# Program-text order on all five engines, and a DFT column transform in 64 x 64 quadrants

## The chip, the core and the metric

The kernel runs on one core of one Trainium2 chip. The metric is the device time of one execution in microseconds. A core has five engines that run side by side, each through a queue of its own: PE (TensorE, matrix multiplies; its weight loads are shown apart as PEld), DVE (VectorE), ACT (ScalarE), POOL (GpSimd) and SP (SyncE, which here only issues transfers). They wait for each other through semaphores. Within one queue the instructions start in the order in which the program was built.

## The reference, cut to what matters

The input is a float32 batch of 32 images of 96 channels and 56 x 56 pixels. Two layers follow.

```
layer 0: h = silu(bn(conv1x1(x, 96 -> 576)));  d = silu(bn(depthwise3x3(h)))
         s = sigmoid(W2 silu(W1 mean(d)));      x1 = x + bn(conv1x1(d * s, 576 -> 96))
layer 1: mag  = |rfft2(x1)|                     (per channel, 56 x 29)
         ca   = gate per channel, from weighted sums of mag
         sa   = gate per pixel, from mean(x1), l2(x1) and the resized mean of mag
         y    = x1 * ca * sa
         fq   = resized mean over channels of |rfft2(y)|
         off, gate = 3x3 convolutions of [y, coordinates, fq]
         z    = (1 - gate) * conv3x3(y) + gate * deformable3x3(y, off)
         out  = relu(batchnorm(z) + x1)
```

Each image needs two DFTs of all 96 channels, one of x1 and one of y. A DFT is a transform of rows and then a transform of columns, both done as matrix products, followed by the square root of the sum of two squares.

## The kernel before

**Streams.** `layers` interleaves three streams by hand. The main loop goes over 32 images x 7 bands of 8 rows; a band is two halves, and each half samples 7 column blocks of 4 x 4 pixels (`sample_tiles`, L714 on PE and its evictions L718 on ACT), packs nine taps into seven (`pack`, L725) and contracts them (`deform`, L733). Beside it run two generators: `hidden` of the image after next (expansion L166, activation L170, nine depthwise taps per unit on DVE at L255 to L259, and `finish`, L219), and `attend` of the next image (squeeze L282 to L294, projection L321 and L327, and all of layer 1 up to `fq`). `pump` is called once for each column block and three times more at the end of a band, so 70 times for an image, and advances both generators so that each is through when it is due; a generator stands still at each `yield`. `later` holds short pieces that are due some slots on.

**Order.** The generators fix the order of the program text. The body of `layers` lies in `tc.manual_schedule(engines={SP})`: SP's queue keeps the text's order, while PE, ACT, DVE and POOL are ordered by a list scheduler, which may move an instruction ahead of or behind its neighbours in the text as far as data allow. One ACT instruction, L663, is pinned to the text by `keep_in_program_order`.

**The two transforms.** `dft_mag` takes two channels at a time. The row transform (L383) multiplies the pixels of a channel pair by `FU`; the result has two channels x 56 columns on 112 partitions in `s1`. The column transform (L404) multiplies `s1` by a block-diagonal 112 x 112 matrix `GV`, which holds the 56 x 56 cosine (or sine) matrix twice and zeros elsewhere. Three steps of 16 channel pairs each make eight matmul records of 464 columns. ACT squares the two results from PSUM (L406), DVE adds them (L407), and one square root over all follows (L410). The buffer `sq` exists once, and in the first DFT it also holds the sums of L369 until L395 has read them.

**The small chain.** After the first DFT come short dependent steps, each waiting for the one before on another engine: `sums` to L470, L471 and L472; `m_fe` (L420) to L423; `mas` and `qs` (L478 to L490) to L494; L500; L505; L512 with L514; L524 to L528; L533 with L534; L540 with L542; L544 to L549. All of the PSUM tiles of this chain come from one pool `acc` with a single buffer.

**Buffers.** Six PSUM banks `mm` rotate among everything else on PE; `pd` exists once.

Of the kernel before, what the change touches and what calls it, by code (L numbers as in the profile page):

```python
# [24 lines left out]
V = W // 2 + 1  # L25
# [35 lines left out]
NG = C // 2 // CG  # L61
KG = 3
# [273 lines left out]
def dft_mag(nc, p, src, gate=None):  # L336

    w = p["w"]
    hwc = src.rearrange("c (h w) -> h c w", h=H)
    s1 = p["s1p"].tile([2 * W, NP, 2 * V], FP, name="s1")
    if gate is None:
        parts = p["sq"].tile([2 * W, 2, NPB * V], FP, name="sq")[:, :, : NG * W].rearrange("p k (g w) -> p k g w", g=NG)  # L350
    x2s = []

    def load(g):
        if g < NG:
            x2 = p["x2"].tile([2 * H, CG, W], FP, name="x2")
            for half in range(2):
                c0 = half * C // 2 + g * CG
                nc.sync.dma_start(x2[half * H : (half + 1) * H], hwc[:, c0 : c0 + CG])
            x2s.append(x2)

    def weigh(g):
        if gate is not None and g < NG:
            nc.gpsimd.tensor_tensor(x2s[g], x2s[g], gate.unsqueeze(1).to_broadcast([2 * H, CG, W]), ALU.mult)

    def sums(g):
        sq = bank(p)[: 2 * H, : CG * W].rearrange("h (c w) -> h c w", c=CG)
        nc.scalar.activation(sq, x2s[g], AF.Square)
        for k, t in enumerate((x2s[g], sq)):
            nc.vector.tensor_reduce(parts[:, k, g], t.rearrange("h c w -> h w c"), AX.X, ALU.add)  # L369

    for g in range(3):
        load(g)
    for _ in range(2):
        yield
    weigh(0)
    weigh(1)
    yield
    if gate is not None:
        yield
    for g in range(NG):  # L380
        pt = bank(p)
        for i in range(CG // 2):
            nc.tensor.matmul(pt[: 2 * W, i * 4 * V : (i + 1) * 4 * V],  # L383
                             x2s[g][:, 2 * i : 2 * i + 2, :].rearrange("h c w -> h (c w)"), w["FU"],
                             start=True, stop=True)
        if gate is None:
            sums(g)
        weigh(g + 2)
        load(g + 3)
        nc.scalar.copy(s1.rearrange("p (h q) u -> p h q u", h=2)[:, :, g * CG // 2 : (g + 1) * CG // 2],  # L390
                       pt[: 2 * W, : 2 * CG * V].rearrange("p (q h u) -> p h q u", h=2, u=2 * V))
        yield
    if gate is None:
        p["sums"] = p["sp"].tile([2 * H, 2, W], FP, name="sums")
        nc.vector.tensor_reduce(p["sums"], parts.rearrange("p k g w -> p k w g"), AX.X, ALU.add)  # L395
    mag = s1[:, :, :V]
    for j in range(0, NP, NPB):
        n = NPB * V
        sq = p["sq"].tile([2 * W, 2, n], FP, name="sq")
        cos, sin = s1[:, j : j + NPB, :V], s1[:, j : j + NPB, V:]  # L400
        for part, first, second in ((0, (0, cos), (1, sin)), (1, (0, sin), (2, cos))):
            pt = bank(p)
            for k, (g, m) in enumerate((first, second)):
                nc.tensor.matmul(pt[: 2 * W, :n].rearrange("p (q u) -> p q u", q=NPB), w["GV"][:, g], m,  # L404
                                 start=(k == 0), stop=(k == 1))
            nc.scalar.activation(sq[:, part], pt[: 2 * W, :n], AF.Square)  # L406
        nc.vector.tensor_tensor(mag[:, j : j + NPB], sq[:, 0].rearrange("p (q u) -> p q u", q=NPB),  # L407
                                sq[:, 1].rearrange("p (q u) -> p q u", q=NPB), ALU.add)
        yield
    nc.scalar.activation(mag, mag, AF.Sqrt)  # L410
    p["magnitude"] = mag


def resized_spectrum(nc, p, mag, name, scale=None):


    m2 = p["sp"].tile([2 * W, V], FP, name=f"m_{name}")
    if scale is not None:
        nc.vector.tensor_tensor(mag, mag, scale.unsqueeze(2).to_broadcast([2 * W, NP, V]), ALU.mult)
    nc.vector.tensor_reduce(m2, mag.rearrange("p q u -> p u q"), AX.X, ALU.add)  # L420
    yield
    pf = p["acc"].tile([128, 512], FP, name="acc")
    nc.tensor.matmul(pf[:V, : 2 * W], m2, p["w"]["RT2"], start=True, stop=True)  # L423
    rs = p["sp"].tile([V, 2, W], FP, name=name)
    nc.scalar.copy(rs.rearrange("p m w -> p (m w)"), pf[:V, : 2 * W])
    p["resized"] = rs
    yield


def attend(tc, p, b, x, h2d, pooled, x1, given=False):  # L430
# [45 lines left out]
    mas = p["sp"].tile([2 * W, 2, NP], FP, name="mas")  # L476
    edge = p["sp"].tile([2 * W, NP, NE], FP, name="edge")
# [3 lines left out]
    for m in range(2):  # L481
        we = p["sp"].tile([2 * W, NP, NE], FP, name="we")
        nc.vector.tensor_tensor(we, edge, w["wa"][:, m], ALU.mult)
        nc.vector.tensor_reduce(mas[:, m], we, AX.X, ALU.add)


    qs = p["sp"].tile([2 * W, 2, 3, NP], FP, name="qs")
    for m in range(2):
        nc.vector.tensor_tensor(qs[:, m], mas[:, m].unsqueeze(1).to_broadcast([2 * W, 3, NP]), w["wb"][:, m], ALU.mult)
# [16 lines left out]
    c2 = p["sp"].tile([2 * MID, 2 * W], FP, name="c2")  # L506
# [5 lines left out]
    nc.tensor.matmul(pc[: 2 * W, 64 : 64 + NP], c2, w["cp2X"], start=True, stop=True)  # L512
    cx = p["sp"].tile([2 * W, NP], FP, name="cx")
    nc.vector.tensor_tensor(cx, pc[: 2 * W, 64 : 64 + NP], w["cp2bX"], ALU.add)  # L514
# [119 lines left out]
def offsets(nc, p, yp, j, top, hid, ybs, hds):  # L634
# [28 lines left out]
    p["tc"].keep_in_program_order(nc.scalar.activation(ht, ht, AF.Abs, bias=w["blk"]))  # L663
# [115 lines left out]
def constants(tc, ctx, a, p, gather=False):  # L779
# [63 lines left out]
    wa = cp.tile([2 * W, 2, NP, NE], FP, name="wa")  # L843
    wb = cp.tile([2 * W, 2, 3, NP], FP, name="wb")
    gb = cp.tile([C, 3], FP, name="gbias")
    with tc.tile_pool(name="l1w", bufs=1) as wp:
# [7 lines left out]
        ap, bp, fdh, fdw = temp("apad", 2 * W), temp("bpad"), temp("fdhX"), temp("fdwX")  # L854
        ta = wp.tile([2 * W, NP, NE], FP, name="ta")
        tb = wp.tile([2 * W, 3, NP], FP, name="tb")
        for m in range(2):
            for d in range(7):
                first = d == 0
                oa, ob = (wa[:, m], wb[:, m]) if first else (ta, tb)  # L860
                nc.vector.tensor_tensor(oa, ap[:, m, d].unsqueeze(1).to_broadcast([2 * W, NP, NE]),
                                        fdh[:, :, d : d + 1].to_broadcast([2 * W, NP, NE]), ALU.mult)
                nc.vector.tensor_tensor(ob, bp[:, m, :, d : d + 1].to_broadcast([2 * W, 3, NP]),
                                        fdw[:, :, d].unsqueeze(1).to_broadcast([2 * W, 3, NP]), ALU.mult)
                if not first:
                    nc.vector.tensor_tensor(wa[:, m], wa[:, m], ta, ALU.add)
                    nc.vector.tensor_tensor(wb[:, m], wb[:, m], tb, ALU.add)
# [41 lines left out]
def padded(nc, p, a, images):  # L909
# [3 lines left out]
    for t in yps:  # L913
        nc.gpsimd.memset(t, 0.0)
        nc.sync.dma_start(t[C : C + 4, PD : PD + H, PD : PD + W], a["coord"])
        nc.sync.dma_start(t[CA:, PD : PD + H, PD : PD + W], a["place"])
    p["s4"] = [cp.tile([H, 3, WP], FP, name=f"s4_{i}") for i in range(2)]
# [11 lines left out]
def layers(tc, a, dp, x1d, zd, stats, far):  # L929
# [8 lines left out]
    with ExitStack() as ctx:  # L938
# [7 lines left out]
        pools(tc, ctx, p, None, (("xt", 2), ("acch", 2), ("pl", 2), ("w3s", 1), ("hq", 1), ("o", 2), ("x2", 3),  # L946
# [290 lines left out]
def gather_block(tc, a, dp, x1d, zd, stats):  # L1237
# [4 lines left out]
    with ExitStack() as ctx:  # L1242
# [11 lines left out]
        pools(tc, ctx, p, None, (("x2", 3), ("ca", 1), ("s1p", 1), ("xc", 2), ("sp", 1), ("sq", 2), ("q1", 2), ("q2", 2),  # L1254
# [77 lines left out]
def body(ctx, tc, a, out):  # L1332
# [8 lines left out]
    with tc.manual_schedule(engines={mybir.EngineType.SP}):  # L1341
# [8 lines left out]
def _arrays(inp):  # L1350
# [39 lines left out]
    A["cp1"] = np.ascontiguousarray(cp1.reshape(2 * MID, 3, NP, 2).transpose(2, 1, 3, 0))  # L1390
    cp2 = l1["cp2_w"].reshape(NP, 2, MID)
    A["cp2X"] = np.ascontiguousarray(cp2.transpose(1, 2, 0).reshape(2 * MID, NP))
    A["cp2bX"] = np.ascontiguousarray(np.repeat(l1["cp2_b"].reshape(NP, 2).T, W, 0))
    A["twoT"] = np.kron(np.eye(2), np.ones((MID, W))).astype(f)
# [8 lines left out]
    for k in range(1, KA):  # L1403
# [13 lines left out]
    A["GV"] = np.ascontiguousarray(np.stack(  # L1417
        [np.kron(two, np.cos(t)), np.kron(two, np.sin(t)), np.kron(two, -np.sin(t))], 1).astype(f))
    A["two"] = np.kron(two, np.ones((W, 1))).astype(f)
# [8 lines left out]
    apad, bpad = np.zeros((1, 2, 7, V), f), np.zeros((2, W, 2, 3, 7), f)  # L1428
    for d in range(7):
# [3 lines left out]
        bpad[:, -np.arange(V), 1, :, d] = bp[:, 6 - d : 6 - d + V].T[:, None]  # L1433
# [4 lines left out]
    A["apad"], A["bpad"] = ends, bpad.reshape(2 * W, 2, 3, 7)  # L1438
    A["bsum"] = np.stack([bp[:, 6 - d : 6 - d + V].sum(1) for d in range(7)], -1).astype(f)[None]
    pairs = lambda v: np.repeat(v.reshape(NP, 2, 7).transpose(1, 0, 2), W, 0)  # L1440
# [7 lines left out]
    RT2 = np.zeros((2, W, 2, W), f)  # L1448
    RT2[:, np.arange(V), 0] = RT / C
    RT2[:, -np.arange(V), 1] = RT / C  # L1450
    A["RT2"] = RT2.reshape(2 * W, 2 * W)
# [37 lines left out]
```

## Time and profile before

| | |
|---|---|
| time, median of 3 runs | 9672.42 us (9670.12 to 9673.45) |
| profiled execution | 9701.68 us; span of its instructions 9699.9 us |
| PE busy | 8626.3 us, 89% of the span |
| DVE busy | 7237.3 us, 75% |
| ACT busy | 5341.9 us, 55% |
| POOL busy | 2531.2 us, 26% |
| mean granted TensorE clock | 0.932 |
| first matmul of `hidden` | at 75.29 us |

A row of a group of instructions gives line, engine, operation, out<-in with shapes and count, then the busy time of the group in us and the mean time of one in ns, then how long the engine had been idle just before them and whose end released it. A float32 matmul stands in the trace as two MATMUL records. Records overlap, so busy time divided by count is less than the mean time of one. The waits list gives engine, line and what it waited for, then the total in us, the number of times and the longest in us. A timeline row gives start, duration and number of records, with the idle time before them in brackets.

### The profile page before, as it was taken

To read this page: it belongs to the slowest core of one execution; us is meant where nothing else is said; L and a number is where in the kernel's file an instruction comes from. 1 tells how busy PE (TensorE), PEld (TensorE's weight loads), DVE (VectorE), ACT (ScalarE), POOL (GpSimd) and SP (SyncE) were. 2 spreads that over 40 slices of the span, in tenths; PEclk is the share of its full clock that TensorE was granted. 3 is DMA by queue.
4 is the path that set the end of the run, shared out by engine and by line. 5 is a ranking of instruction groups with operands and counts; after the bars stand their busy time and mean duration, and the time that the engine had idled before them with its cause. 6 is when DMAs were issued, how large, how long until landed. Compare 5 with 4: busy or idle time off the path is not lost. (4 is left out here: it accounts for less than half of the span.)

```text
span 9699.9 us, 120622 instructions
## 1 busy us (share of the span) xinstructions
PE 8626.3 (89%) x43766; PEld 5004.7 (52%) x43766; DVE 7237.3 (75%) x6948; ACT 5341.9 (55%) x10262; POOL 2531.2 (26%) x2639
## 2 busy tenths in 40 slices
PE   6889999999999999999999999999999999999970
PEld 3455555555555555555555555555555555555540
DVE  7688777777877777787777787777778777777323
ACT  2355555555555556555555555555555555555453
POOL 0133222222222232222222222233222223322210
PEclk9899999999999999999999999999999999999985
DMA  2345555554555555555555555555545555554449
GB/s 94 107 136 143 160 153 157 157 153 138 140 158 152 157 149 148 140 144 150 153 158 154 139 139 155 153 157 155 152 138 143 151 157 157 153 146 135 128 152 417
DMA packets 1069310, 1485.39 MB, mean 153 GB/s; under 512 B 590406, under 2 KB 839958, under 8 KB 1056422
## 3 DMA queue, kind: packets, MB, share of 16 engines
q1 hardware_dynamic: 858747, 985.20, 37.3%
q10 hardware_dynamic: 153675, 329.79, 9.1%
q0 software_dynamic: 56288, 162.60, 6.8%
q8 instruction: 352, 5.77, 0.3%
q14 instruction: 248, 2.03, 0.1%
HBM read 1064.28 MB, written 412.65 MB: 152 GB/s over the span
## 5 line engine op out<-in xcount | busy, mean ns | idle before, releaser
L259 DVE SCALAR_TENSOR_TENSOR acch<-hp,w,acch 128x1512 f32<-128x1512 f32 (+1 forms) x2250 | 4314.4, 1918 | 32.8
L598 PE MATMUL mm<-yp,c_jointW 104*128 104x448 f32 x4032 | 1648.5, 561 | 6.2 <-DMA yp<-fqd 3.4
L733 PE MATMUL pd<-v,c_def 128*96 128x224 f32 (+1 forms) x6272 | 1435.2, 380 | 174.5 <-ACT v L725 147.9
L696 POOL COPY ybl<-yp 96x448 f32<-96x448 f32 x896 | 1016.6, 1161 | 2002.3 <-PE mm L700 1996.8
L733 PEld LDWEIGHTS pd<-v,c_def 128*96 128x96 f32 (+1 forms) x6272 | 1065.3, 175 | 487.7 <-ACT v L725 186.7
L166 PE MATMUL mm<-xt,w 96*128 96x392 f32 (+3 forms) x2688 | 1117.2, 553 | 132.6 <-ACT yt L702 95.9
L714 PE MATMUL mm<-wc,yt 64*96 64x144 f32 x12544 | 1113.9, 301 | 119.1 <-ACT v L718 59.3
L598 PEld LDWEIGHTS mm<-yp,c_jointW 104*128 104x128 f32 x4032 | 785.1, 196 | 802.7 <-issue 760.1
L685 DVE TENSOR_TENSOR wc<-wc,wr 128x1008 f32<-128x1008 f32 x448 | 559.3, 1248 | 776.4 <-DMA wr<-hd 767.9
L219 ACT ACTIVATE acch<-acch,sh,inv 128x1568 f32<-128x1568 f32 x288 | 487.4, 1692 | 1159.2 <-DVE acch L259 1141.5
L714 PEld LDWEIGHTS mm<-wc,yt 64*96 64x96 f32 x12544 | 847.7, 162 | 442.9 <-issue 197.7
L718 ACT COPY v<-mm 96x288 f32<-96x288 f32 (+1 forms) x2688 | 1003.1, 441 | 127.9 <-PE mm L714 85.6
L170 ACT ACTIVATE hp<-mm,sh,inv 128x392 f32<-128x392 f32 (+2 forms) x1216 | 811.6, 672 | 329.4 <-PE mm L166 280.8
L626 PE MATMUL mm<-yp,c_base0W 96*64 96x448 f32 x4032 | 914.6, 551 | 0.0
L321 PE MATMUL mm<-hq,w3s 128*96 128x392 f32 x2048 | 789.9, 532 | 126.5 <-DMA hq<-h2d 124.2
L648 POOL DMA_DIRECT2D od<-at x224 | 185.9, 830 | 2257.6 <-DVE at L644 1483.9
L725 ACT COPY v<-v 32x448 f32<-32x448 f32 x1344 | 755.1, 562 | 29.7
L404 PE MATMUL mm<-s,c_GV 112*112 112x464 f32 x1536 | 662.9, 573 | 0.0
L166 PEld LDWEIGHTS mm<-xt,w 96*128 96x128 f32 (+1 forms) x2688 | 390.5, 187 | 513.8 <-issue 289.8
L702 ACT COPY yt<-mm 128x384 f32<-128x384 f32 (+1 forms) x896 | 351.1, 441 | 463.9 <-PE mm L700 462.0
L321 PEld LDWEIGHTS mm<-hq,w3s 128*96 128x96 f32 x2048 | 336.9, 173 | 478.6 <-issue 374.4
L626 PEld LDWEIGHTS mm<-yp,c_base0W 96*64 96x64 f32 x4032 | 295.3, 135 | 527.8 <-issue 487.9
(193 smaller groups left out, 8959.1 us busy)
## 6 DMA issues: line engine op xcount, KB each, us to landing
h2d<-acch ACTq DMA_DIRECT2D x288, 784.0 KB
wc<-hd SPq DMA_DIRECT2D x896, 252.0 KB
wr<-hd SPq DMA_DIRECT2D x896, 252.0 KB
hq<-h2d SPq DMA_DIRECT2D x128, 980.0 KB
hq<-h2d SPq DMA_DIRECT2D x128, 784.0 KB
x<-x1d SPq DMA_DIRECT2D x768, 98.0 KB
ht<-od SPq DMA_DIRECT2D x224, 252.0 KB
hd<-ht ACTq DMA_DIRECT2D x224, 252.0 KB
```

Of the source, the lines that this page charges most:

```text
L166: nc.tensor.matmul(pt[p0 : p0 + w1.shape[1], : rows * W], w1, xts[hf][:, r0 * W : (r0 + rows) * W], start=True, stop=True)
L170: nc.scalar.activation(h1[lo:hi, row0 : row0 + rows, 1 : 1 + W], pt[lo:hi, : rows * W].rearrange("p (h w) -> p h w", h=rows), AF.Silu, bia ...
L259: nc.vector.scalar_tensor_tensor(acc[:, lo:hi], win, wk, acc[:, lo:hi], ALU.mult, ALU.add)
L321: nc.tensor.matmul(pts[half][:C, :EW], w3s[:, ch], hq, start=(i == 0), stop=False)
L404: nc.tensor.matmul(pt[: 2 * W, :n].rearrange("p (q u) -> p q u", q=NPB), w["GV"][:, g], m, start=(k == 0), stop=(k == 1))
L598: nc.tensor.matmul(view, weights[:, k], yp[:channels, r0 : r0 + RB, dx + PD - 1 : dx + PD - 1 + W], start=(k == 0), stop=(k == NTAP - 1))
L626: nc.tensor.matmul(pb[k % 2 * BC : (k % 2 + 1) * BC, :BW].rearrange("p (h w) -> p h w", h=RB), w["base"][:, k], yp[:C, r0 : r0 + RB, dx + ...
L696: nc.gpsimd.tensor_copy(yb[:, :, s], blocks)
L714: nc.tensor.matmul(pt[k][:C, (t - lo) * KP : (t - lo + 1) * KP], yt[ps, t], s[ps, t * KP : (t + 1) * KP], start=True, stop=True)
L718: nc.scalar.copy(v[:C, :, lo:hi, k].rearrange("c k t p -> c t k p"), pt[k][:C, : (hi - lo) * KP].rearrange("c (t k p) -> c t k p", t=hi - ...
L725: nc.scalar.copy(v[C:, 1 + 2 * i : 3 + 2 * i], v[i * QC : (i + 1) * QC, KA:])
L733: nc.tensor.matmul(out.rearrange("c q (t x) -> c t q x", x=TS), p["w"]["def"][ks, k], v[ks, k].rearrange("c t s (r x) -> c t (s r) x", r=T ...
```

## The change

It does two things.

First, `manual_schedule` is called without a set of engines, so that PE, ACT, DVE and POOL, too, keep the order of the program text. The pin on L663 goes, since it says the same. The text itself, with its yields and slots, stays, but for what follows.

Second, the column transform is done in quadrants. `s1` gets 2 x 64 partitions in place of 2 x 56; the source buffers `x2` are padded to 64 columns with zeros and are kept for the whole program, in place of a pool of three. `GV` becomes a plain 56 x 56 matrix (padded to 64) on either half of the partitions. Each step takes 2 x 2 groups of 8 channel pairs; a matmul uses 64 rows and 64 columns of the array and 232 moving columns, and four of them that follow each other lie in four different quadrants. The two row halves write two different PSUM banks. A step has 16 matmuls (32 records) in place of 4 (8 records), and there are three steps as before (in the diff NQB = 8 and WX = 64). The squares, the sums of squares, the square root and all that is computed from `mag` run on 128 partitions in place of 112, with constants ordered to match.

```diff
-        x2 = p["x2"].tile([2 * H, CG, W], FP, name="x2")
+        x2 = p["x2"][p["n_x2"] % len(p["x2"])]
+        p["n_x2"] += 1
...
-    for j in range(0, NP, NPB):
-        n = NPB * V
-        sq = p["sq"].tile([2 * W, 2, n], FP, name="sq")
-        cos, sin = s1[:, j : j + NPB, :V], s1[:, j : j + NPB, V:]
-        for part, first, second in ((0, (0, cos), (1, sin)), (1, (0, sin), (2, cos))):
-            pt = bank(p)
-            for k, (g, m) in enumerate((first, second)):
-                nc.tensor.matmul(pt[: 2 * W, :n].rearrange("p (q u) -> p q u", q=NPB), w["GV"][:, g], m,
-                                 start=(k == 0), stop=(k == 1))
-            nc.scalar.activation(sq[:, part], pt[: 2 * W, :n], AF.Square)
-        nc.vector.tensor_tensor(mag[:, j : j + NPB], sq[:, 0].rearrange("p (q u) -> p q u", q=NPB),
-                                sq[:, 1].rearrange("p (q u) -> p q u", q=NPB), ALU.add)
+    n = NQB * V
+    pairs = mag.rearrange("p (r q) u -> p r q u", r=2)
+    for q0 in range(0, NP // 2, NQB):
+        sq = p["sq"].tile([2 * WX, 2, 2, n], FP, name="sq")
+        pts = bank(p), bank(p)
+        for part, first, second in ((0, (0, 0), (1, V)), (1, (0, V), (2, 0))):
+            for t, (g, u0) in enumerate((first, second)):
+                for r, k in ((0, 0), (1, 1), (0, 1), (1, 0)):
+                    rows = slice(r * WX, r * WX + W)
+                    q1 = k * NP // 2 + q0
+                    nc.tensor.matmul(pts[r][k * WX : (k + 1) * WX, part * n : (part + 1) * n].rearrange("p (q u) -> p q u", q=NQB),
+                                     w["GV"][rows, g], s1[rows, q1 : q1 + NQB, u0 : u0 + V], start=(t == 0), stop=(t == 1))
+        for r, pt in enumerate(pts):
+            nc.scalar.activation(sq[:, r].rearrange("p k n -> p (k n)"), pt[:, : 2 * n], AF.Square)
+        nc.vector.tensor_tensor(pairs[:, :, q0 : q0 + NQB], sq[:, :, 0].rearrange("p r (q u) -> p r q u", q=NQB),
+                                sq[:, :, 1].rearrange("p r (q u) -> p r q u", q=NQB), ALU.add)
...
-    p["tc"].keep_in_program_order(nc.scalar.activation(ht, ht, AF.Abs, bias=w["blk"]))
+    nc.scalar.activation(ht, ht, AF.Abs, bias=w["blk"])
...
-    with tc.manual_schedule(engines={mybir.EngineType.SP}):
+    with tc.manual_schedule():
         layers(tc, a, dp, x1d, zd, stats, far)
```

Lines move by 2 in `hidden`, by 3 in the row transform and by 7 from `resized_spectrum` to the constants: L166 becomes L168, L219 L221, L404 L410, L406 and L407 L413 and L414, L420 L427, L512 L519, L524 L531, L533 L540, L540 L547, L714 L721, L725 L732, L733 L740.

## The prediction

> **What bounds the kernel now.** I read the page's engine rows first, then the row of the granted clock, the groups by line, PE's waits, and the timeline of one image. Engines and clock:
>
> ```profile
> PE 8626.3 (89%) x43766; PEld 5004.7 (52%) x43766; DVE 7237.3 (75%) x6948; ACT 5341.9 (55%) x10262; POOL 2531.2 (26%) x2639
> PEclk9899999999999999999999999999999999999985
> ```
>
> PE is busy 8626 of 9700 us. Its last matmul ends at about 9411 and its first starts at 75.29; in between it idles about 695 us, 21.5 us for each of 32 images. PE is the bound, so two things can move the time: its work, and its holes. DVE at 75% has slack on average, but a wait behind two or three of its long instructions is long. The clock row never says 10: in the records the clock is full or half, half for about 30 us per image, after holes of 2 to 5 us. Now the groups that the change touches or resembles:
>
> ```profile
> L598 PE MATMUL mm<-yp,c_jointW 104*128 104x448 f32 x4032 | 1648.5, 561 | 6.2 <-DMA yp<-fqd 3.4
> L714 PE MATMUL mm<-wc,yt 64*96 64x144 f32 x12544 | 1113.9, 301 | 119.1 <-ACT v L718 59.3
> L626 PE MATMUL mm<-yp,c_base0W 96*64 96x448 f32 x4032 | 914.6, 551 | 0.0
> L404 PE MATMUL mm<-s,c_GV 112*112 112x464 f32 x1536 | 662.9, 573 | 0.0
> ```
>
> Busy divided by count: L404 takes 0.432 us per record of 464 columns. L598, of nearly L626's columns with the whole array, takes 0.409; L626, with two column halves side by side, takes 0.227, a factor of 0.555. And PE's longest waits:
>
> ```profile
> PE pd L733 <- ACT v L725: 147.9, 71, 6.9
> PE mm L321 <- DMA hq<-h2d: 124.2, 30, 7.9
> PE mm L166 <- ACT yt L702: 95.9, 40, 5.4
> PE acc L423 <- DVE m_fe L420: 43.9, 32, 1.9
> PE acc L524 <- DVE cx L514: 23.7, 29, 1.4
> ```
>
> Waits behind ACT are waits for ACT's order. The small chain costs almost nothing: 1.4 us per image at L423, 0.7 at L524. The timeline of PE shows why:
>
> ```profile
> 4257.65 0.47 PE L700 MATMUL mm<-c_ident,ybl 96*128 96x96 f32 x3 [0.88 <-ACT sq L406]
> 4262.63 1.68 PE L166 MATMUL mm<-xt,w 96*128 96x392 f32 x2 [2.03 <-ACT yt L702]
> 4265.46 0.55 PE L423 MATMUL acc<-c_RT,m_fe 112*29 112x112 f32 x2 [1.16 <-DVE m_fe L420]
> ...
> 4292.59 0.31 PE L524 MATMUL acc<-thT,s 56*56 56x56 f32 x2 [0.39 <-DVE cx L514]
> 4292.83 1.00 PE L733 MATMUL pd<-v,c_def 128*96 128x224 f32 x4
> 4293.76 0.30 PE L524 MATMUL acc<-thT,s 56*56 56x56 f32 x2
> 4293.99 1.00 PE L733 MATMUL pd<-v,c_def 128*96 128x224 f32 x4
> ```
>
> Between two steps of the chain the scheduler has put a matmul of another stream, so ACT evicts the one step while PE works.
>
> **The quadrants.** They remove L404's 662.9 us. There are now 64 DFTs x 3 steps x 32 = 6144 records of 232 columns. One alone should take 0.432/2 = 0.216, so without overlap the work doubles to 1327. Two at a time, with L626's factor: 0.120 each, 737 in all, 74 more than now. Four at a time, with 0.28, about half that factor: 0.060 each, 370 with some 35 us for the switches of tile shape around each step (64 x 3 x 2 switches at 0.09 us; around L714 the first group of a new shape starts 211 ns after the last in place of 122). Gain 293, at best 331.
>
> A rule speaks against this. L626's column halves share all their rows, and its records pair off without an exposed weight load. The Trainium skill, "TensorE: Matmul & The Clock Gate" (What overlaps and what doesn't), says that a weight load passes a running matmul only if their row groups differ. Here two of the four quadrants share a row group, and weights change at every matmul. By the rule about 0.07 us of load would stand bare in each record and the quadrants would cost nearly 6144 x 0.13 = 800, a loss of about 140; by L626's row they gain. I take the row: same rows, loads of the same size, nothing exposed. The switch itself is a drain by "TensorEngine Tiling (Array Packing)" (Key Properties), which gives no figure; the 0.09 us of the trace is used.
>
> ACT's squares stay 2 x 3 per DFT, DVE's sums too; more partitions cost no time. -293.
>
> **The order, start.** ACT's constant loads now stand in text order: some that were issued at 2.6 us come behind two square roots and 19 more loads. SP's first `xt` load waits for `thM`, now built by one chain of DVE steps rather than by interleaved ones. First matmul at 95 to 100 us in place of 75.29: +22.
>
> **The order, after the first DFT.** (Lines here and below are those of before.) In the text PE's next work, a hidden unit's expansion and L423, stands behind L420, DVE's reduction. DVE has ahead of it, from the last L369 on: the four steps of `z` (0.68, 0.80, 0.66, 0.62, each starting before the last ends, 2.2 in all), L395 1.3, three L407 at 0.6, one L685 at 1.2, six taps L259 at 1.95 and one L257 at 1.0 (12.7), then L420 2.6. That is 21.8; small instructions between them 1.0, and waits for ACT's squares 1.5: 24.3. PE's own work over that stretch is 13.9. So PE stands 10.4 us there, once per image (between 5 and 14: how far DVE is ahead when the stretch begins decides). Before, the same stretch has 0.88 + 0.27 + 2.03 + 1.16 = 4.3. In steady state there are 31 images: 31 x 6.2 = +192.
>
> **The order, around the resize of the gates.** In the text L505, L512, two L524, L526 and L527 stand in one block on PE, then one L166 and six L714, then three L533, nine L540 and L549 in one block. No deformable contraction lies between them as it did in the timeline above. Each waits for ACT's eviction of the one before, from a single `acc` buffer. And ACT in the text has L219 and more between the last L528 and the first L534. Step by step, by rows of before: rest of a DVE tap 1.5; the `z` chain ahead of `cx` on DVE 2.7 with its waits; L514 0.2; two L524 with their evictions L528, 0.31 + 0.30 twice, and L515's 0.24, 1.4; L526 and L527 with theirs 0.8; on ACT L219 1.69 + 0.19, L170 0.68, three L725 at 0.56 and two L718 at 0.4 to 0.5, 5.1; three evictions L534 0.9; the last three L540 and L542 0.8; two L546 0.5: 13.9. Ten hops from engine to engine at 0.24 (L524's matmul ends at 4292.90, its eviction starts at 4293.19) make 16.3. PE's own work is 3.6. Stall 12.7 us (9 to 16), before 0.4: 31 x 12.3 = +381.
>
> **Other waits.** New: the second L423 after its own reduction (1.2), the squeeze L288 (0.5), L700 behind POOL's L696 (2.4), less some 1.4 that go: 31 x 2.6 = +80 (0 to 150). Gone: L733's wait for L725 (147.9), since in the text the packs stand where they are needed; and of L166's for `yt` and L714's for `v`, outside the stretch above, some 70: -218 (-100 to -350). The wait of L321 for `hq` (124) is one for data by DMA; SP's order is unchanged, and I leave it.
>
> **The clock.** A hole of 3.46 us slowed the next L321 from 2.87 to 4.54 us:
>
> ```profile
> 5027.84 2.87 PE L321 MATMUL mm<-hq,w3s 128*96 128x392 f32 x8
> 5035.86 4.54 PE L321 MATMUL mm<-hq,w3s 128*96 128x392 f32 x8 [3.46 <-DMA hq<-h2d]
> ```
>
> Holes go and others come; I take nothing, and +-104 (3.3 us an image) for the range. The tail of 288 us after PE (the normalisation) has one order by data in both: nothing.
>
> **Sum.** -293 + 22 + 192 + 381 + 80 - 218 = +164 us. The profiled execution took 9701.7, 0.3% above the median of 9672.42; the sum is put on the median: 9836.
>
> **Rivals.**
> Faster: the stalls of the two stretches are mostly covered. My sums add worst order to worst order, but an engine that PE no longer feeds catches up, and DVE and ACT may enter each stretch ahead. With 14 us an image fewer of stalls, or with half of that and a better clock, the time is about 9480. For it: ACT is busy 55% only. Against: the blocks stand back to back in the text, and no lead helps a chain that goes through PE, ACT and PE. The point that decides: new stalls, less those that go, of 9 us per image (293/31).
> Quadrants in pairs only, by the rule: +74 to +140 in place of -293, so 10200 to 10270 with the order's cost.
> Clock: PE comes out of each of the two stretches at half clock and stays there; 8 us more an image, about 10100.
> Even: the costs of order just eat the quadrants.
> The change may also not do what it says in one point: the 64-row quadrants could leave PE limited by ACT's squares (0.55 us for each of six); at 3.3 us per DFT against 5.8 of PE this binds only in a step's last part, and is in the range.
>
> **How the numbers follow.** My forecast, a loss of about 1 to 3.5%, 0.49; faster, 0.29; even, 0.05; pairs only, 0.07; the clock, 0.10. So slower has 0.66. The likeliest one's own range is 9700 to 10000; the range that leaves no more than 2 in 10 out reaches into the faster case and to the clock case: 9560 to 10130. 0.2% (19 us) is about what a measurement of this kernel can tell from none.
>
> **What would show it** (lines of the changed kernel, 2 to 7 higher). Right: L410 busy about 370 us (in place of L404's 663); a wait of PE's L430 for DVE's L427 of about 8 us, 32 times; waits of L531 for `cx` and for ACT's L535, of L540 and L547 for ACT's L541 and L549, about 12 us an image together; L740's wait for L732 near nothing; first matmul at 95 to 100 us. Wrong: L410 busy over 660 (the rule on weight loads held); the two stretches without holes over 3 us; or a granted clock well below 0.93, which would say that the holes cost more than their length.

## The result, and the profile after

| | before | after |
|---|---|---|
| time, median | 9672.94 us | 10564.02 us |
| ratio, 95% interval | | 1.0922 (1.0905 to 1.0939) |
| span of the profiled execution | 9699.9 us | 10570.9 us |
| PE busy | 8626.3 us | 8768.3 us |
| PE's waits, sum of the list | 781 us | 1500 us |
| granted clock, mean | 0.932 | 0.877 |

The kernel became 891 us slower, five times the forecast loss of 164, and outside the range. Slower was forecast; the size was not. The engine and clock rows of the changed kernel's page:

```profile
PE 8768.3 (83%) x48374; PEld 5260.1 (50%) x48374; DVE 7321.6 (69%) x6948; ACT 5376.8 (51%) x10262; POOL 2305.0 (22%) x2642
PEclk9888898888888888889898888989888898888895
```

PE is busy longer, although the quadrants took 272 us from it, and the clock row now shows 8 where it showed 9. Both suggest that PE did the same other work more slowly. PE's groups that matter (line, tile, shapes, count, then busy us and mean ns, then the idle time before and what ended it), first the row transform as it was before (L383):

```profile
L383 PE MATMUL mm<-c_FU,x 112*112 112x116 f32 x3072 | 418.1, 285 | 55.2 <-POOL x L363 37.9 <-DMA x<-x1d 17.2
```

Then the changed kernel's costliest group (L605, before L598 with 1648.5 us), its row transform and its quadrants:

```profile
L605 PE MATMUL mm<-yp,c_jointW 104*128 104x448 f32 x4032 | 1750.1, 591 | 51.2 <-DMA yp<-fqd 42.8 <-ACT v L732 3.0 <-ACT v L725 2.7
...
L386 PE MATMUL mm<-c_FU,x 112*128 112x116 f32 x3072 | 478.6, 308 | 279.2 <-DMA x<-x1d 271.9 <-issue 3.2 <-POOL x L366 3.0
L410 PE MATMUL mm<-s,c_GV 56*64 56x232 f32 x6144 | 391.2, 379 | 23.1 <-ACT hp L172 21.4 <-ACT sq L413 1.7
```

L410 costs 391.2/6144 = 0.064 us per record: the four quadrants do run side by side, as forecast (0.060). But the row transform went from 418.1 to 478.6, and L605 took 102 more. PE's waits in the changed kernel:

```profile
PE mm L386 <- DMA x<-x1d: 271.9, 31, 10.3
PE acc L430 <- DVE m_fe L427: 230.0, 32, 8.3
PE mm L707 <- POOL ybl L703: 181.0, 72, 8.5
PE acc L430 <- DVE m_fy L427: 96.2, 31, 9.0
PE acc L540 <- ACT s L541: 84.4, 64, 2.5
PE acc L531 <- DVE cx L521: 72.9, 32, 2.4
...
PE pd L740 <- ACT v L732: 24.3, 37, 1.7
```

The second, fourth, fifth and sixth lines were forecast, and so was the last (147.9 before). The first was not, nor the size of the third. Before, those two were:

```profile
PE mm L383 <- DMA x<-x1d: 17.2, 3, 12.0
...
PE mm L700 <- POOL ybl L696: 2.6, 1, 2.6
```

One image in PE's timeline, holes in brackets, shows the two forecast stretches and the hole at the row transform ahead of them:

```profile
4317.66 2.03 PE L386 MATMUL mm<-c_FU,x 112*128 112x116 f32 x8 [8.79 <-DMA x<-x1d]
...
4367.01 0.55 PE L430 MATMUL acc<-c_RT,m_fe 128*29 128x112 f32 x2 [7.50 <-DVE m_fe L427]
...
4393.98 0.43 PE L531 MATMUL acc<-thT,s 56*56 56x56 f32 x2 [2.41 <-DVE cx L521]
4394.81 0.43 PE L531 MATMUL acc<-thT,s 56*56 56x56 f32 x2 [0.39 <-ACT t L535]
...
4403.33 0.34 PE L540 MATMUL acc<-twT,t 56*56 56x56 f32 x2 [2.47 <-ACT s L541]
```

And DVE's timeline, ahead of the hole at L430 and, in the first four rows, ahead of the hole at L386:

```profile
4308.85 1.21 DVE L692 TENSOR_TENSOR wc<-wc,wr 128x1008 f32<-128x1008 f32 x1 [3.93 <-DMA wr<-hd]
4309.97 3.73 DVE L261 SCALAR_TENSOR_TENSOR acch<-hp,w,acch 128x1568 f32<-128x1568 f32 x2
4313.62 0.90 DVE L372 TENSOR_REDUCE sq<-x 112x56 f32<-112x448 f32 x1
4314.44 0.62 DVE L372 TENSOR_REDUCE sq<-mm 112x56 f32<-112x448 f32 x1
...
4359.54 1.20 DVE L692 TENSOR_TENSOR wc<-wc,wr 128x1008 f32<-128x1008 f32 x1
4360.66 3.73 DVE L261 SCALAR_TENSOR_TENSOR acch<-hp,w,acch 128x1568 f32<-128x1568 f32 x2
4364.31 2.56 DVE L427 TENSOR_REDUCE m_fe<-s 128x29 f32<-128x1392 f32 x1
```

At L430 it is the forecast picture: taps and one L692 stand ahead of L427. At L386 it is the same cause one step removed. DVE waits 3.93 us for `wr`, then does two taps, and only then L372, the last reader of an x2 buffer. SP's load of the next group into that buffer starts at 4314.67, and PE goes on at 4317.66:

```profile
4314.67 2.15 SPq L361 DMA_DIRECT2D x<-x1d  x4
```

The waits of SP's queue say the same of the whole run. Its loads of `x` waited for L372 614 us in all, where before (L358 for L369) they had waited 8 us. Before, and in the changed kernel:

```profile
SPq L358 <- DVE sq L369: 8.3, 4, 2.6
```

```profile
SPq L361 <- DVE sq L372: 613.9, 98, 15.3
```

**The account** of the profiled executions, 871 us: quadrants -272; row transform +60 (L383 to L386); PE's waits +718; all else that PE is busy with, +354; the other 11 are mostly the tail after PE's last matmul (297 in place of 289).

The +354 go with the half clock: in the trace's clock record PE ran at half clock, up to its last matmul, for 1038 us before and 2318 us after. The trace allows a check that depends on no other run. Give each matmul record the time by which it lengthens PE's busy time, and sort the records by the clock at which they start. At full clock L605 then takes 384 ns per record, as L598 did (385); at half clock it takes 731, and the records that start there went from 189 to 497. Over all this other work the full-clock price accounts for a net 2 us of the growth, and what the half-clock records cost above it for 339.

### The profile page after: what moved, and what is told of

Read it like the earlier page. It is cut to its first block, busy times and chain, and to the rows that moved or that the text cites. A ratio compares the mean times of both kernels' runs of the same rounds, so it can differ in the third digit from the quotient of the medians.

```text
span 10570.9 us, 129774 instructions
## 1 busy us (share of the span) xinstructions
PE 8768.3 (83%) x48374; PEld 5260.1 (50%) x48374; DVE 7321.6 (69%) x6948; ACT 5376.8 (51%) x10262; POOL 2305.0 (22%) x2642
## 5 line engine op out<-in xcount | busy, mean ns | idle before, releaser
L261 DVE SCALAR_TENSOR_TENSOR acch<-hp,w,acch 128x1512 f32<-128x1512 f32 (+1 forms) x2250 | 4249.3, 1889 | 51.9 <-ACT hp L172 1.2
L605 PE MATMUL mm<-yp,c_jointW 104*128 104x448 f32 x4032 | 1750.1, 591 | 51.2 <-DMA yp<-fqd 42.8
L740 PE MATMUL pd<-v,c_def 128*96 128x224 f32 (+1 forms) x6272 | 1443.7, 386 | 43.5 <-ACT v L732 24.3
L740 PEld LDWEIGHTS pd<-v,c_def 128*96 128x96 f32 (+1 forms) x6272 | 1107.6, 180 | 413.7 <-issue 121.8
L605 PEld LDWEIGHTS mm<-yp,c_jointW 104*128 104x128 f32 x4032 | 831.5, 208 | 943.2 <-issue 819.8
L168 PE MATMUL mm<-xt,w 96*128 96x392 f32 (+3 forms) x2688 | 1203.0, 590 | 94.4 <-DMA xt<-in_x 45.3
L721 PE MATMUL mm<-wc,yt 64*96 64x144 f32 x12544 | 1117.4, 314 | 60.6 <-ACT hp L172 38.2
L692 DVE TENSOR_TENSOR wc<-wc,wr 128x1008 f32<-128x1008 f32 x448 | 605.9, 1352 | 750.9 <-DMA wr<-hd 750.8
L721 PEld LDWEIGHTS mm<-wc,yt 64*96 64x96 f32 x12544 | 884.0, 174 | 401.2 <-issue 241.3
L725 ACT COPY v<-mm 96x288 f32<-96x288 f32 (+1 forms) x2688 | 1002.2, 443 | 155.8 <-PE mm L721 111.6
L703 POOL COPY ybl<-yp 96x448 f32<-96x448 f32 x896 | 873.8, 1004 | 652.9 <-PE mm L707 652.9
L651 DVE COPY at<-mm 18x224 f32<-18x224 f32 x448 | 154.4, 380 | 994.9 <-ACT hid L625 987.8
L323 PE MATMUL mm<-hq,w3s 128*96 128x392 f32 x2048 | 769.2, 521 | 75.8 <-DMA hq<-h2d 59.5
L709 ACT COPY yt<-mm 128x384 f32<-128x384 f32 (+1 forms) x896 | 352.9, 442 | 909.1 <-PE mm L707 903.9
L732 ACT COPY v<-v 32x448 f32<-32x448 f32 x1344 | 755.2, 562 | 26.5 <-ACT acch L221 0.4
L386 PE MATMUL mm<-c_FU,x 112*128 112x116 f32 x3072 | 478.6, 308 | 279.2 <-DMA x<-x1d 271.9
L386 PEld LDWEIGHTS mm<-c_FU,x 112*128 112x128 f32 x3072 | 442.2, 217 | 403.0 <-issue 334.6
L221 ACT ACTIVATE acch<-acch,sh,inv 128x1568 f32<-128x1568 f32 x288 | 488.3, 1696 | 289.0 <-DVE acch L261 287.0
L466 POOL TENSOR_TENSOR o<-o,xc 96x392 f32<-96x392 f32 x256 | 331.8, 1296 | 1379.8 <-ACT o L333 1372.0
```

Source lines behind the costliest of these rows:

```text
L168: nc.tensor.matmul(pt[p0 : p0 + w1.shape[1], : rows * W], w1, xts[hf][:, r0 * W : (r0 + rows) * W], start=True, stop=True)
L261: nc.vector.scalar_tensor_tensor(acc[:, lo:hi], win, wk, acc[:, lo:hi], ALU.mult, ALU.add)
L323: nc.tensor.matmul(pts[half][:C, :EW], w3s[:, ch], hq, start=(i == 0), stop=False)
L386: nc.tensor.matmul(pt[:, i * 4 * V : (i + 1) * 4 * V], x2s[g][:, 2 * i : 2 * i + 2, :].rearrange("h c w -> h (c w)"), w["FU"], start=True, ...
L605: nc.tensor.matmul(view, weights[:, k], yp[:channels, r0 : r0 + RB, dx + PD - 1 : dx + PD - 1 + W], start=(k == 0), stop=(k == NTAP - 1))
L703: nc.gpsimd.tensor_copy(yb[:, :, s], blocks)
```

## The experiments

Runs of different sessions are compared by their medians; `before` stood between 9663 and 9677 us in all of them.

**1. The two parts one by one.** `quads` is the changed kernel with `engines={SP}` and the pin put back; `order` is before with `manual_schedule()` for all engines and without the pin.

```diff
-    with tc.manual_schedule():
+    with tc.manual_schedule(engines={mybir.EngineType.SP}):
```

> The quadrants alone: the column transform of the changed kernel, the order of before (SP in text order, the other four engines ordered by the list scheduler, the pin kept). Theory (the parts add up: the quadrants save what L410's busy time shows, the order costs the rest): L410 near 391 us as in the changed kernel, against 663, the other groups and PE's waits as before, so 9672 - 272 = 9400 us (9360 to 9460), granted clock 0.93. Rival (the quadrants themselves hurt: two PSUM banks taken at once and 16 matmuls in a row hold up the other streams, and part of the loss is theirs): 9600 us or more, with new PE waits around L410.

> The order alone: before's column transform, all five engines in text order. Theory (parts add up): the changed kernel's 10564 plus the 272 us that the quadrants saved: 10836 (10750 to 10930), half-clock time and the waits of L423, L383 and L700 as large as the changed kernel's. Rival (part of the loss belongs to the quadrants): below 10600 us.

Measured: quads 9663.57 us, ratio to before 0.9997 (0.9983 to 1.001); order 10608.12, ratio 1.0966 (1.0934 to 1.0997). The order makes the whole loss, +938; with it the quadrants bring 44 us (the intervals of the two ratios just touch), and in the list's order nothing. Both expectations that the 272 us would show were wrong. Nor do they bring their 267 us in text order: from `order` to the changed kernel the column transform falls from 658.2 to 391.2, but the row transform rises by 54 (424.5 to 478.6) and PE's other work by 165, while half clock goes from 2048 to 2318 us. PE's waits stay (1499 and 1500). Why the half clock grows with the quadrants is open. In the list's order, three lines of `quads` say where they went, two groups and a wait:

```profile
L386 PE MATMUL mm<-c_FU,x 112*128 112x116 f32 x3072 | 465.0, 301 | 48.8 <-POOL x L366 31.2 <-DMA x<-x1d 17.4
L410 PE MATMUL mm<-s,c_GV 56*64 56x232 f32 x6144 | 372.0, 375 | 0.6 <-ACT sq L413 0.6
PE mm L707 <- ACT sq L413: 80.4, 26, 6.2
```

L410 saves 291. L386 takes 47 of it back. All other groups together grow by 101 (L721 alone by 46), at 1219 us of half clock in place of 1038. PE's waits grow by 86: L707 waits 80 us for ACT's squares (10 before), L430 84 (50 before). What is left is 55 us between two profiled executions, and nothing between the medians.

**2. One queue at a time.** First one queue given back to the list (the others in text order), then one queue alone in text order (the others by the list), then PE and DVE given back together. The edit is the set of engines:

```diff
-    with tc.manual_schedule():
+    with tc.manual_schedule(engines={SP, PE, Activation, Pool}):    (dve_list)
+    with tc.manual_schedule(engines={SP, DVE, Activation, Pool}):   (pe_list)
+    with tc.manual_schedule(engines={SP, Activation, Pool}):        (pe_dve_list)
+    with tc.manual_schedule(engines={SP, PE}):                      (pe_text; the other three alike)
```

> The changed kernel with DVE alone given back to the list scheduler; PE, ACT, POOL and SP stay in text order. Theory (DVE's place in the text makes the holes at L430, 326 us, and at L386, 272 us, where L372 releases the x2 buffers late): both waits fall below 100 us together, some 450 us of holes go, and with them the half clock that follows, some 150: 9950 us (9800 to 10100). Rival (the holes come from where PE's own blocks stand in the text, whatever DVE does): 10350 or more.

> The changed kernel with PE alone given back to the list scheduler; DVE, ACT, POOL and SP stay in text order. Theory (PE stands in holes because DVE and ACT deliver late, but it has other work that it could do there): PE's waits fall from 1500 to some 900 us, time 9900 (9700 to 10150). Rival (what PE could do instead hangs on the same late DVE and ACT queues): 10350 or more. If it is below 9500, the order of DVE and ACT costs nothing by itself.

> The quadrants with PE alone (and SP, as always) in text order; DVE, ACT and POOL by the list scheduler. Beside quads (all four by the list, 9664) and the changed kernel (all in text order, 10564). Theory (PE's own blocks make the loss): 10150 us or more (10100 to 10450), with the waits of L430, L531 and L540. Rival (PE's order is harmless while the other queues can run ahead): under 9850.

> The quadrants with DVE alone in text order. Theory (PE's blocks make the loss, DVE only delivers): 9664 to 9800. Rival (DVE's queue, with its long taps and the waits of L692 and L372 in it, holds up the rest whatever PE does): 10000 or more. If each queue alone costs under 150 and all together 900, the loss is a coupling: the list of one queue goes round the holes of another.

> The quadrants with ACT alone in text order. Theory (PE's blocks make the loss): 9600 to 9750, and L740's wait for L732 falls from 101 us to near nothing as it does in the changed kernel, so it may even gain. Rival (ACT's text order holds evictions back, as L221 ahead of L541): 9900 or more.

> The quadrants with POOL alone in text order. Theory (PE's blocks make the loss): 9664 to 9720. Rival (POOL's issues of sad and od stand in its queue ahead of L703 and L366, and PE's 181 us at L707 come from there): 9830 or more, with that wait above 150 us.

> The changed kernel with PE and DVE given back to the list scheduler; ACT, POOL and SP in text order. If the queues' costs were separate, this would bring 46 + 217 = 263 us: 10300. If they are coupled (each of the two in text order forces its places on the other), what is left is the cost of ACT and POOL in text order, 177 and 199 us alone: 9840 to 10040.

| | us | against |
|---|---|---|
| quads (none in text order) | 9664 | |
| pe_text | 10413 | +750 on quads |
| dve_text | 10007 | +344 |
| act_text | 9840 | +177 |
| pool_text | 9862 | +199 |
| after (all) | 10564 | +900 |
| dve_list | 10518 | -46 on after |
| pe_list | 10347 | -217 |
| pe_dve_list | 9926 | -638 |

The four alone add up to 1470, all together cost 900; giving back DVE and PE one at a time brings 46 (not told apart from none: the intervals overlap) and 217, both together 638 and not 263. So the cost of the order is no sum over queues. The reading that fits is that a queue in text order forces its places on the ones that wait for it, so that one queue that may choose is of little use while the others may not.

Of the seven expectations, two were met. PE's own text order is the dearest by itself (`pe_text`), and giving back PE and DVE leaves about what ACT and POOL in text order cost (`pe_dve_list`). The theory that PE's blocks alone make the loss fell: in `dve_text` and `pool_text` its rivals came true, and in `dve_list` too the rival's figure did. `pe_list` (10347) lies at the edge of its rival, 10350. `act_text` was expected between 9600 and 9750 and missed: L740's wait for L732 rose to 268 us instead of vanishing. The longest waits of PE in `act_text` and in `pool_text`:

```profile
PE pd L740 <- ACT v L732: 268.1, 62, 8.8
```

```profile
PE mm L707 <- POOL ybl L703: 289.4, 116, 13.8
```

`dve_list` shows how a hole moves. Its waits of PE:

```profile
PE acc L430 <- DVE m_fe L427: 231.0, 28, 9.3
PE mm L605 <- DMA yp<-fqd: 219.2, 30, 9.3
PE mm L323 <- DMA hq<-h2d: 198.8, 30, 9.2
...
PE mm L386 <- DMA x<-x1d: 23.2, 23, 10.2
```

The hole at L386 closed, 272 to 23 us, as the reading of L372 said. L430's stayed: the list itself now put five taps between the last L414 and L427. And L605 and L323 wait 316 us longer for their loads, so that the sum of waits is 1591 in place of 1500.

**3. Single holes.** `ring4` gives the changed kernel a fourth x2 buffer, `yields` spreads the small chain in the text, `fill` puts work without use into PE's holes. (To make room for the buffer, `ring4` also lets two small tiles, `qs` and `c2`, share the space of others.)

```diff
-    [cp.tile([2 * H, CG, WX], FP, name=f"x2_{i}") for i in range(3)]
+    [cp.tile([2 * H, CG, WX], FP, name=f"x2_{i}") for i in range(4)]          (ring4)
...
     nc.scalar.activation(t1[:, m], t, AF.Identity, bias=w["sdh_b"](m, W))
+        yield                                                                (yields, in six places)
...
+    for _ in range(25 if name == "fe" else 10):                              (fill, ahead of L430)
+        nc.tensor.matmul(pf[:V, : 2 * W], p["w"]["RT2"][:, :V], p["w"]["RT2"], start=True, stop=True)
```

> The changed kernel with a fourth x2 buffer (two small tiles share the room of others, qs with we and c2 with t1, to make place for it). Theory (each hole of PE has its own price): PE's 272 us at L386 for x<-x1d come from the third buffer, which L372 releases late; they fall below 60, and the half clock after that hole goes with them, some 100: 10250 us (10150 to 10350). Rival (the pace is set by a chain through several queues, a hole that is closed opens elsewhere, as with DVE in the list's order): 10450 or more, with the sum of PE's waits within 100 us of 1500.

> The changed kernel with more yields in attend, so that the text spreads the small chain: two more between L427 and L430, two after cx, one after each step of L531, L540 and L547, one ahead of L556. All five engines stay in text order. Theory (each hole has its own price, and the stretches' blocks make these): the waits of L430 (326 us), L519, L531, L540, L547 and L556 (about 290) fall below 150 together; with the half clock, 10564 - 460 - 150 = 9950 (9850 to 10150). Rival (a chain through several queues sets the pace): 10350 or more, other waits grow.

> The changed kernel with idle-time work for PE: 25 more small matmuls (112 columns, result overwritten) ahead of L430 for fe, 10 ahead of L430 for fy, 10 behind L519, 10 ahead of L540; nothing else. They fill part of PE's holes there, some 11 us an image. Theory (holes cost more than their length, since the half clock that follows them slows the next work): half-clock time falls by 20 us an image of 65, time 10400 (10300 to 10480), although PE has more to do. Rival (the half clock costs nothing, PE waits again later anyway): 10564 to 10650.

`ring4`: 10375.85 us, 188 faster than the changed kernel, about 60% of what was expected. The wait for `x<-x1d` fell from 272 to 10 us, but a part of it stands there under other names:

```profile
PE mm L386 <- ACT s L393: 104.2, 30, 5.3
...
PE mm L168 <- DVE sq L372: 52.6, 29, 2.1
```

Half-clock time fell from 2318 to 2038 us with it. So the late release of the third buffer is shown as a cause of 188 us. That it is DVE's L372 that holds it is read from the trace; `dve_list` agrees, where SP's wait for L372 fell from 614 to 3 us and L386's closed.

`yields`: 11107.55 us, 544 slower. The waits of L430 are gone from the top of its list, as expected, but:

```profile
PE mm L709 <- POOL ybl L705: 584.1, 118, 13.4
PE acc L502 <- DVE qs L498: 327.4, 32, 10.9
```

(In this kernel L703 is L705, L707 is L709 and L501 is L502.) The edit did more than was meant. `pump` (called 119 times for an image by the code: 7 bands of 14 column blocks and three more, not the 70 said above) spreads the steps of `attend` evenly over an image, so more yields in two places pull all other steps closer together. `qs` is now used too soon behind its making, and the loads and POOL's weighing crowd each other (POOL waits 445 us for `x`, 188 in the changed kernel). This is the likely reading of the two lines, and no run tests it. It is no clean trial of the two stretches; it does show that slack added in one place of this text was paid for in others.

`fill`: 10502.46 us, 62 faster, although PE does 430 us more (groups of the useless matmuls: 280.1, 80.2 and 69.7). PE's waits fell by 237, to 1262. Its other work fell from 8768 to 8522 us, by 246, as half-clock time fell from 2318 to 1720: 0.4 us of PE's time for each us of half clock. The sum, 430 - 237 - 246 = -53, is the span's change. So the theory was right in sign: a hole costs more than its length, though 62 us is less than the 164 that was expected, and the time lies just above the theory's range.

**4. Why the quadrants bring nothing in the list's order.** `quads_less` and `before_less` leave out the second term of each sum of the column transform, `quads_split` squares each half when it is complete, `quads_ring4` and `before_ring4` have a fourth x2 buffer, `quads_cols` is `quads_ring4` with a row transform in column halves without padding. (The two that leave out a term do not compute the reference's spectra; they serve as a price of PE's work only.)

```diff
-            for t, (g, u0) in enumerate((first, second)):
+            for t, (g, u0) in enumerate((first,)):                            (quads_less; before_less alike)
...
+            for r, pt in enumerate(pts):                                      (quads_split, in the loop over part)
+                nc.scalar.activation(sq[:, r, part], pt[:, part * n : (part + 1) * n], AF.Square)
...
+            for k in range(2):                                                (quads_cols, in place of L386)
+                nc.tensor.matmul(pt[k * WX : (k + 1) * WX, i * 4 * V : (i + 1) * 4 * V],
+                                 x2s[g].rearrange("h c w -> h (c w)")[:, (2 * i + k) * W : (2 * i + k) * W + WX], w["FU"],
+                                 start=True, stop=True)
```

> The quadrants in the list scheduler's order with half of their matmuls left out (the second term of each sum, so the spectra are not the reference's): PE has 186 us less to do. Theory of the prediction (PE is the bound): 9664 - 186 = 9480 us (9430 to 9530). Rival (in the list's order a chain through DVE's taps and the loads of wr sets the pace, and PE's time is no longer its price): 9620 to 9680, with PE's waits up by about 150.

> Before, with half of the column transform's matmuls left out (the second term of each sum, so the spectra are not the reference's): L404 falls from 663 to some 331 us. Theory (PE is the pace in the list's order, and the quadrants' missing gain was eaten by costs of their own): 9670 - 330 = 9340 (9290 to 9400). Rival (less PE work brings less than its time, whichever way it is taken): 9480 or more.

> The quadrants in the list's order, with four squares of 232 columns per step in place of two of 464: the first two start when the first half of the matmuls is done. Theory (two banks held to the end of a step make PE wait, 80 us at L707 for L413 and more at L430): that wait falls below 30, time 9600 (9560 to 9640). Rival (ACT's 384 more instructions cost as much, or the wait only moves): 9650 to 9720.

> The quadrants in the list's order with a fourth x2 buffer. In the changed kernel the fourth buffer brought 188 us. Theory (in the list's order the third buffer is not what PE waits for; L386 waits 49 us in all): 9620 to 9665. Rival (the buffers are a coupling that costs in any order): 9560 or less.

> Before with a fourth x2 buffer. L383 waits 55 us in all in before. Expected 9610 to 9670; below 9600 only if the buffers also hold up DVE or POOL.

> quads_ring4 with the row transform in two column halves of 64 (as L633 does), each of its own 56 columns of x2 and 8 that are not used, so that x2 needs no padding: 6144 records of 116 columns in place of 3072. Theory (the padding made the weights, not the moving columns, the limit of L386; halves that run side by side hide it): L386 falls from 428 us of start-to-start time to 320 to 380, time 9641 - 30 to 60 = 9580 to 9610. Rival (two half loads cost what one whole load costs, or the shape switches cost it): L386 at 420 or more, time 9640 to 9700.

`quads_less`: 9428.70 us, 235 less than quads. `before_less`: 9455.87, 210 less than before, where L404 fell by 312 (662.9 to 351.3). The rows of the two:

```profile
L410 PE MATMUL mm<-s,c_GV 56*64 56x232 f32 x3072 | 222.8, 405 | 2.1 <-ACT sq L413 2.1
```

```profile
L404 PE MATMUL mm<-s,c_GV 112*112 112x464 f32 x768 | 351.3, 579 | 0.1
```

So PE's work does have a price in the list's order: 0.67 of its time in `before_less`, and more than its time in `quads_less`, where L410 fell by 149 (372.0 to 222.8) and PE's waits by 90. The rival that PE no longer sets the pace fell. By the lower rate the quadrants' 291 were worth about 200, as an estimate, and their side costs ate these. `before_less` falls short of the 330 that were expected because PE's other work grew by 85 us (L733 alone by 65, 1435.2 to 1499.8). PE's waits did not grow in sum (776 against 781), though L714's for DVE's `yb` went from 39 to 87.

`quads_split`: 9853.26 us, 190 slower than quads and beyond both expectations. The wait of L707 for L413 went, and a larger one came, since the second half of a step's matmuls goes into the banks that ACT is still reading:

```profile
PE mm L410 <- ACT sq L413: 323.4, 138, 9.3
```

`quads_ring4`: 9641.08, ratio to before 0.9978 (0.9967 to 0.9989); `before_ring4`: 9650.28, 0.9984 (0.9973 to 0.9995). The fourth buffer helps both a little, and the quadrants' own share, 9 us, lies within the intervals. `quads_ring4` is 0.2% faster than before, the fastest median here with the reference's computation, but not told apart from `before_ring4`. `quads_cols`: 9677.39, 0.9994 (0.9983 to 1.0006). The row transform in halves is busy 440.0 us in place of 470.2 in `quads_ring4`, a little over half the way back to 418, and the time did not fall. So the padding is real as a cost of PE, but its removal in this way gains nothing.

Not settled is which of the quadrants' side costs weighs most in the list's order: padding (47), ACT's squares that come only at the end of a step (80 at L707), half clock. The list reorders all queues with each edit, and each trial moved more than one of them.

## Why the prediction was wrong, point by point

- **The quadrants' row, -293.** Right as a row (-291 in `quads`, -272 in the changed kernel), wrong as a price. The prediction took a fall of PE's busy time to be a fall of the time. Missing was the padding of x2 to 64 columns, which makes the row transform's weights 128 columns in place of 112: with the clock full its records start 122 ns apart in place of 109, a ratio near 128/112. Not all of its +60 is that: 583 of its 3072 records start at half clock, 368 before. Missing too was that two banks come free together at the end of a step. That more partitions cost no time held: a square (L413) takes 554 ns on 128 partitions, 552 on 112.
- **The rule on weight loads.** L626's row was the better guide: with the clock full, L410's records start 57 ns apart in `quads`, and the rule weighed there (the Trainium skill, "TensorE: Matmul & The Clock Gate", What overlaps and what doesn't) would have them at 130, by the prediction's estimate. The rival of pairs fell with it.
- **Start, +22.** First matmul at 103.22 in place of 75.29: +28.
- **After the first DFT, +192.** L423's waits, 50.3 us, became L430's, 326.2: +276. Per image the first L430 stood 7.2 us, where 10.4 were forecast, and the second 3.0, where 1.2 were. Their sum, 10.2, is near 10.4 by chance. (The row of the sum also took 4.3 us an image off for the holes of before; here these stand under the waits that go.)
- **Resize of the gates, +381.** Waits of L519, L531, L533, L540, L547 and L556: 276 us, against 32 before: +244, or 8.6 us an image where 12.7 were forecast. DVE and ACT came to the stretch less late than the sum of rows had it: where 5.1 us of ACT's work and three evictions were put ahead of L540 and L547, L540 waited 2.6 us an image.
- **Other waits, +80: the first step that failed.** L386 for `x<-x1d` +255, L707 for POOL +178 (forecast 2.4 us an image, 74). The prediction left loads by DMA alone, on the ground that SP's order is unchanged (it said so of L321's `hq`), and had no term for `x`. It asked who issues a load and not who frees its buffer: L372, late in DVE's text order, for which SP's loads waited 614 us in place of 8. With a fourth buffer the time fell by 188 us.
- **Waits that go, -218.** Right in kind, -290 in size: L733's fell by 131, L714's and L321's by 109, L166's behind its first load by 50. L321's part, 51, was not forecast.
- **The clock, 0: the other step that failed, by as much.** PE's other work took 354 us more, for 1280 us more of half clock. The prediction's own two rows showed the price of one hole: L321 took 1.67 us more behind 3.46 us of waiting. The prediction had the rival (8 us an image; it was 11) at one in ten, and its sum let holes that go and holes that come cancel, though by the same sum the new ones outweighed the old by 435 us.

Put right term by term, the forecast of 164 becomes 164 + 21 (row of the quadrants) + 60 (row transform) + 6 (start) + 84 (after the first DFT) + 353 (other waits) - 137 (resize of the gates) - 72 (waits that go) + 354 (clock) = 833, of the 871 us between the two profiles; the rest is small waits and the tail. `fill` and the split of records by clock show the clock's part, `ring4` the third buffer's. For POOL's part `pool_text` gives 289 us of that wait with POOL alone in text order; what holds POOL up there was not tried.

The prediction's own sums hold but for small slips: 10.4 less 4.3 is 6.1 and not 6.2, the other waits add up to 2.7 us an image and not 2.6, PE idles 710 us and not 695 between the two times it names, and 14 us an image fewer of stalls would give 9402 and not 9480. None of them changes the outcome.

## What to carry to other kernels

A fall of an engine's busy time is a price only after three questions: what does the new layout cost its neighbours (here padding, banks), is the engine's time the pace, and what clock will it have. When a scheduler's order is replaced, look for each new wait at who frees the buffer, not only at who issues the load; and do not add up costs queue by queue, since they are coupled. Price a new hole on PE above its length, by what the trace shows for the work behind such holes.

## What was not expected of the hardware

In the changed kernel's clock record, 234 of the 259 stretches at half clock begin behind 3.4 us in which PE was busy for less than 70%, and they last 3.4, 6.8, 10.2 us and so on up to 24, 9 us in the mean. The converse holds in the main: of the stretches of 3.4 us into which the full-clock time falls, 313 had PE busy for less than 70%, and 235 of these were the last before half clock; of the other 1987 only 25 were. That fits the window of about 3.4 us that "TensorE: Matmul & The Clock Gate" of the Trainium skill names (Part 1). The "<1% of a typical kernel span" that the same page gives for the ramp is said of the warm-up at the start, and is no price for a kernel that falls back to half clock 259 times: at 0.28 us per us (354 for 1280) to `fill`'s 0.4, 2318 us of half clock are, as an estimate from these two, 650 to 930 us, 6 to 9% of the span. In `fill`, useless matmuls in the holes paid for more than half of themselves (246 of 430 us) through the clock.
